# Masked attention in one kernel: scores kept in SBUF, row maxima spread by DMA, the mask as a bias

## The chip, the cores and the metric

The kernel runs on one core of a Trainium2 chip. The metric is the device time of one execution in microseconds. The core has five engines that run their own instruction streams and wait for each other by semaphores: TensorE (PE, with its weight loads PEld), VectorE (DVE), ScalarE (ACT), GpSimd (POOL) and SyncE (SP), which here only issues DMA transfers. Matrix products land in PSUM, which has eight banks of 128 partitions x 512 float32; everything else lives in SBUF. All data are float32.

## What is computed

Four layers follow each other, each added to its input x of shape 8 x 256 x 512: a masked attention (L0), a modulated attention (L1), an oscillator scan over 256 time steps (L2) and a GRU scan (L3). The change concerns the first, and where the result of the second is kept:

```python
def _L0_cond_ref(x, mask, Wq, Wo):          # x: B=8, D=256, T=512; mask: 8 x 512 of 0 and 1
    xt = jnp.transpose(x, (0, 2, 1))
    q = xt @ Wq.T
    qh = q.reshape(B, T, NH, dk).transpose(0, 2, 1, 3)           # 8 heads of 32
    scores = scale * jnp.einsum('bhqd,bhkd->bhqk', qh, qh)
    logits = (scores * cmask + (1.0 - cmask) * NEG) * rmask      # NEG = -1e30
    attn = jax.nn.softmax(logits, axis=-1)
    ctx = jnp.einsum('bhqk,bhkd->bhqd', attn, qh)
    out = ctx.transpose(0, 2, 1, 3).reshape(B, T, D) @ Wo.T
    return jnp.transpose(out, (0, 2, 1))
...
x = x + _L0_cond_ref(x, cond_2048, L0_cond_Wq, L0_cond_Wo)
x = x + _L1_cond_ref(x, cond_2048[:, None, :], ...)     # x after this line is called x2 below
x = x + _L2_cond_ref(cond_2048, cond_2048, x, ...)
x = x + _L3_cond_ref(cond_2048, x, ...)
```

Queries, keys and values are the same matrix, so the scores of a head are symmetric. A query row with mask 0 has logits that are all 0, and its result is the mean of all values.

## The kernel before

**Stages.** `tile_kernel` makes small constants, runs `attention` (L0 and L1 of all eight batch entries, interleaved), and then `scans` (L2 and L3). The scans need the weights `cT`, `wih`, `whh`, which `scan_weights` loads, and `x2T`, the result of L1 turned so that features lie on partitions. `x2T` is allocated at the top (L917), 32 KB of each partition, and lives through the whole kernel.

**Steps.** The attention is a software pipeline over steps g (L453 to L515), emitted in the order of the text; each engine runs its instructions in that order. A batch entry b takes U = 8 steps of masked work: two halves e of four heads each, and four steps per half. `at(g, rel, n)` says whether step g is the part number r of entry b at the offset rel; `heads(g, rel)` does so for the four head groups of the modulated attention. `norms`, `parts`, `HEADS` and `OUT` say at which steps an entry's normalization, qkv products, heads and output come.

**Masked attention of one half (b, e).** 
- `project` (steps -5 and -4): q for four heads into a bank; VectorE multiplies it by the mask row `mks` into `qm`, ScalarE copies it into `qt`, and `project_out` turns that on TensorE into `qtok`, the values. On GpSimd a line `neg` is made from the mask.
- `maxima0` (four steps from -4): for one block of 128 queries the scores of four heads over all 512 keys go into four banks (L204), and VectorE takes each row's maximum (L209) into `mxp0`. The condition is copied beside it by GpSimd (L195).
- `rows0`: TensorE turns `mxp0` into rows (L214), and ScalarE writes them, with signs, into `mrow` (L216).
- `weights0` (four steps from 0): the scores again, with keys on partitions, 256 queries at a time (L226), and a second product of depth 2, `neg` by `mrow`, that adds the mask term and subtracts the maximum in the bank (L231). ScalarE takes the exponential from PSUM into `ex` (L238).
- `values0`, in two parts, at steps 1 and 2: `ex` by the values, and `ex` by ones for the sums (both L153); `weigh0`: reciprocal (L163) and product (L164) into `ctxT`.
- `masked_out`: the output projection (L261), added to x on VectorE (L264).

**Modulated attention.** `normalize`, `modulate`, `qkv`, `qkv_norm`, `qkv_out`, `maxima1`, `rows1`, `weights1`, `values1`, `modulated_out`, and `modulated_turn`, which turns x2 on TensorE and copies it into `x2T` (L418). In `qkv_norm` VectorE sums squares (L322), GpSimd takes the power and multiplies (L324 to L326), and `qkv_out` of the next step turns the result. In `values1`, `weigh` follows at once.

**PSUM and queues.** `bank` hands out seven banks in rotation (`ps_s`), one more is for `values0` (`ps_c`). A product waits until the bank's last reader is done. Transfers are issued by SP in order: `load` brings x (four buffers) and the mask spread over 128 partitions, `mks` (one buffer). After step U*B+1 = 65 the pools of the masked attention are closed and `follow` issues the loads of the scan weights.

Of the kernel before, what the change touches and what calls it, by code (L numbers as in the profile page):

```python
# [24 lines left out]
def attention(ctx, tc, cst, x, cond, wqT, woT, w_emb, b_emb, g_norm, w_qkv, g_q, g_k, w_out, x2T, follow):  # L25
# [27 lines left out]
    ps_s = ctx.enter_context(tc.tile_pool(name="a_ps_s", bufs=7, space=PSUM))  # L53
# [7 lines left out]

    xs, mks = {}, {}

    def load(b):
        xs[b] = two.tile([P, 2, D], F32, tag="x", name=f"x_{b}", bufs=4)
        nc.sync.dma_start(xs[b], x[b].rearrange("(k p) t -> p k t", p=P))
        mks[b] = fone.tile([P, D], F32, tag="mk", name=f"mk_{b}")
        nc.sync.dma_start(mks[b], cond[b].partition_broadcast(P))
# [35 lines left out]

    rowm = wp.tile([P, 3], F32, name="rowm")
    nc.vector.memset(rowm, 0.0)
    nc.vector.memset(rowm[:, 1:2], 1.0)
    nc.vector.memset(rowm[:, 2:3], -1.0)
    for h in range(4):
        nc.vector.memset(rowm[32 * h : 32 * h + 1, 0:1], NEG)  # L110
        nc.vector.memset(rowm[32 * h : 32 * h + 1, 1:2], -NEG)
        nc.vector.memset(rowm[32 * h : 32 * h + 1, 2:3], 1.0)
# [54 lines left out]
    qms, qtoks, negs, mrows, exs0, ctxTs = {}, {}, {}, {}, {}, {}  # L167

    def project(b, e):
        if e == 0:  # L170
            qms[b] = ftwo.tile([P, 2, D], F32, tag="qm", name=f"qm_{b}")
            qtoks[b] = ftwo.tile([P, NJ, 256], F32, tag="qtok", name=f"qtok_{b}")
            negs[b] = ftwo.tile([P, D], F32, tag="neg", name=f"neg_{b}")
# [7 lines left out]
        nc.scalar.copy(qt, ps)  # L181
        if e == 0:
            nc.gpsimd.tensor_scalar(negs[b], mks[b], rowm[:, 0:1], rowm[:, 1:2], ALU.mult, ALU.add)
# [7 lines left out]

    def maxima0(b, e, qc):

        if qc == 0:
            nc.gpsimd.tensor_copy(  # L195
                mxp0[e].rearrange("p q (h i) -> p q h i", i=32)[:, :, :, 0],
                condT[:, :, b].unsqueeze(2).to_broadcast([P, NJ, 4]),
            )
        qm = qms[b]
        ss = []  # L200
        for h in range(4):
            r = 32 * h
            s = bank([P, D], f"n0_{b}_{e}_{qc}_{h}")
            nc.tensor.matmul(  # L204
                s, lhsT=qm[r : r + 32, e, qc * P : (qc + 1) * P], rhs=qm[r : r + 32, e, :], start=True, stop=True
            )
            ss.append(s)
        for h in range(4):
            nc.vector.tensor_reduce(mxp0[e][:, qc, 32 * h + 1 : 32 * h + 2], ss[h], AX.X, ALU.max)  # L209

    def rows0(b, e):
        pt = bank([P, NJ, P], f"pm0_{b}_{e}")
        for qc in range(NJ):
            nc.tensor.transpose(pt[:, qc, :], mxp0[e][:, qc, :], ident)  # L214
        mrows[b, e] = ftwo.tile([P, D], F32, tag="mrow", name=f"mrow0_{b}_{e}")
        nc.scalar.activation(mrows[b, e], pt.rearrange("p q n -> p (q n)"), AF.Copy, scale=rowm[:, 2:3])  # L216

    def weights0(b, e, qh, kp):
        qm, neg, mrow = qms[b], negs[b], mrows[b, e]
        qs = slice(256 * qh, 256 * qh + 256)  # L220
        ss = [bank([P, 2, 256], f"s0_{b}_{e}_{qh}_{kp}_{h}") for h in range(4)]
        for i in range(2):
            kc = slice((2 * kp + i) * P, (2 * kp + i + 1) * P)
            for h in range(4):
                r = 32 * h
                nc.tensor.matmul(  # L226
                    ss[h][:, i, :], lhsT=qm[r : r + 32, e, kc], rhs=qm[r : r + 32, e, qs], start=True, stop=False
                )
            for h in range(4):
                r = 32 * h  # L230
                nc.tensor.matmul(  # L231
                    ss[h][:, i, :], lhsT=neg[r : r + 2, kc], rhs=mrow[r : r + 2, qs], start=False, stop=True
                )
        exs = exs0.setdefault((b, e, qh), [])
        exs.append([])
        for h in range(4):
            ex = ftwo.tile([P, 2, 256], F32, tag="ex", name=f"ex0_{b}_{e}_{qh}_{kp}_{h}", bufs=12)
            nc.scalar.activation(ex, ss[h], AF.Exp, scale=SC)  # L238
            exs[-1].append(ex)

    pc0s = {}

    def values0(b, e, qh, half):
        if half == 0:
            if (e, qh) == (0, 0):
                ctxTs[b] = fone.tile([P, 2, D], F32, tag="ctxT", name=f"ctxT_{b}")
            pc0s[b, e, qh] = ps_c.tile([P, 2, 256], F32, tag="c", name=f"pc0_{b}_{e}_{qh}")
        pc = pc0s[b, e, qh]
        o = e * P
        values(pc, half, lambda k, h: qtoks[b][:, k, o + h * DH : o + (h + 1) * DH], exs0[b, e, qh])  # L250

    def weigh0(b, e, qh):
        pc = pc0s[b, e, qh]
        weigh(pc, ctxTs[b][:, e, qh * 256 : (qh + 1) * 256], f"0_{b}_{e}_{qh}")
# [159 lines left out]
    def modulated_turn(b, m, x2):  # L414
# [3 lines left out]
        nc.scalar.copy(x2T[:, :, b, m * P : (m + 1) * P], pt)  # L418
# [6 lines left out]
    for b in range(B):  # L425
        per = 2 if b >= B - 2 else 1
        norms.append(U * b + U + (1 if b == B - 1 else 2))
# [24 lines left out]
    with tc.manual_schedule():  # L452
        for g in range(-5, OUT[-1] + 3):  # L453
# [8 lines left out]
            if a := at(g, 0, U):  # L462
# [539 lines left out]
```

## Time and profile before

| | us |
|---|---|
| median of three runs | 3042.3 (3041.54 to 3044.32) |
| profiled execution | 3040.15 |
| its span, first to last instruction | 3038.4 |
| first product of the scans (L698) | 961.4 |
| first and last copy of masked rows (L216) | 24.5 and 783.4 |
| scan weights issued (L524) | 838.1 |

A row of the page's list of groups reads: line, engine, operation, result and operands by the names of the program, shapes and number; then busy time, the mean duration of one in ns; then the idle time of that engine before them and what ended it. A row of a timeline starts with its start and length in us. A row of a table of windows has the stretch and its length, then for PE, PEld, DVE, ACT and POOL the busy us and the number of instructions, then the granted TensorE clock (1.00 is full), the busy share of the 16 DMA engines and GB/s. "Entry" is a batch entry.

Some groups of the attention stage, by the same profile: L163 64 times 1750 ns, L164 64 times 424 ns, L238 256 times 603 ns, L209 256 times 683 ns, L325 32 times 2899 ns, L326 32 times 1047 ns, L363 32 times 399 ns.

### The profile page before, as it was taken

The page shows a single profiled execution, that of the slowest core. Times are in us where ns is not written, and L with a number is a line of the kernel's source. Part 1 is how long each engine was busy: PE and PEld are TensorE (multiplying, and loading weights), DVE is VectorE, ACT ScalarE, POOL GpSimd, SP SyncE. Part 2 cuts the span into 40 slices and gives each one's busy share as a digit, 9 for nine tenths or more (in the row PEclk, how much of TensorE's full clock was granted, in tenths as well). Part 3 has the DMA queues.
Part 4 walks back from the last instruction along what each step waited for, and adds up shares of the span by engine and source line. Part 5 has one row for each costly group of instructions (what it writes and reads, how often), then busy time and mean ns, then how long its engine had stood idle before and what let it go on. Part 6 is the DMA issues. An engine that isn't in the chain of part 4 may idle for free.

```text
span 3038.4 us, 165918 instructions
## 1 busy us (share of the span) xinstructions
PE 2847.2 (94%) x70330; PEld 2070.0 (68%) x70330; DVE 2002.5 (66%) x9090; ACT 1599.9 (53%) x8347; POOL 986.8 (32%) x2905
## 2 busy tenths in 40 slices
PE   8999999999988899999999999999999999999997
PEld 5455555555545677777777777777777777777775
DVE  4444444544434677777777777777777777777774
ACT  2333433433433566666666666666666666666652
POOL 0021111111221344444444444444444444444442
PEclk8999999999999999999999999999999999999999
DMA  3000000000040000000000000000000000000000
GB/s 129 5 1 1 12 11 1 12 11 1 2 98 2 4 7 6 7 6 6 7 6 7 6 6 7 6 7 6 6 7 6 7 6 6 7 6 7 6 6 7
DMA packets 17759, 35.31 MB, mean 12 GB/s; under 512 B 2144, under 2 KB 10860, under 8 KB 17012
## 3 DMA queue, kind: packets, MB, share of 16 engines
q1 hardware_dynamic: 17012, 24.69, 3.0%
q8 instruction: 550, 9.01, 1.2%
q14 instruction: 197, 1.61, 0.2%
HBM read 20.49 MB, written 4.19 MB: 8 GB/s over the span
## 4 chain that ended last, share of the span: by engine, by line
PE 62%; DVE 26%; ACT 6%; issue 4%; POOL 2%; ACTq 0%; DMA 0%; SPq 0%; POOLq 0%; DVEq 0%
PE pg L733 19%; PE ic L698 17%; PE psqkv L301 5%; DVE icT L890 5%; PE pc L153 5%; DVE qn L891 5%; ACT tT L598 4%; DVE hqs L851 3%; PE s L226 3%; DVE own L748 3%; DVE sqmm L847 2%; PE n L204 2%; DVE v L750 2%; PE psx L401 2%; DVE mxp L209 2%
## 5 line engine op out<-in xcount | busy, mean ns | idle before, releaser
L698 PE MATMUL ic<-cT_sb,tT 128*8 128x128 f32 x32736 | 1088.6, 273 | 82.2 <-ACT tT L598 44.6
L698 PEld LDWEIGHTS ic<-cT_sb,tT 128*8 128x8 f32 x32736 | 758.6, 89 | 344.0 <-ACT tT L598 272.0
L733 PE MATMUL pg<-whh_sb,hz 128*32 128x128 f32 x24576 | 818.5, 274 | 50.7 <-DVE hz L778 17.5
L598 ACT ACTIVATE tT<-qn 128x16 f32<-128x16 f32 x2046 | 440.2, 216 | 646.0 <-DVE qn L891 567.5
L733 PEld LDWEIGHTS pg<-whh_sb,hz 128*32 128x32 f32 x24576 | 667.4, 110 | 125.0 <-DVE hz L778 124.8
L890 DVE STREAM_TRANSPOSE icT<-ic 128x64 f32<-128x64 f32 x2048 | 503.7, 246 | 70.5 <-PE ic L698 64.9
L891 DVE SCALAR_TENSOR_TENSOR qn<-icT,hqs 128x16 f32<-128x16 f32 x2048 | 350.4, 171 | 70.1
L693 POOL TENSOR_TENSOR W<-W,cx 128x128 f32<-128x128 f32 x765 | 297.2, 389 | 256.7 <-ACT cx L679 256.7
L686 POOL TENSOR_TENSOR W<-cx,us 128x128 f32<-128x128 f32 x255 | 117.1, 459 | 446.1 <-ACT cx L679 446.1
L847 DVE SCALAR_TENSOR_TENSOR sqmm<-sqmm,qn 128x32 f32<-128x32 f32 x768 | 153.5, 200 | 152.2 <-ACT sqmm L836 123.1
L209 DVE TENSOR_REDUCE mxp<-n 128x1 f32<-128x512 f32 x256 | 158.7, 683 | 132.0 <-PE n L204 132.0
L851 DVE TENSOR_TENSOR hqs<-W,sqmm 128x32 f32<-128x32 f32 x1020 | 200.1, 196 | 46.1 <-DVE own L773 1.0
L238 ACT ACTIVATE ex<-s 128x512 f32<-128x512 f32 x256 | 132.1, 603 | 157.0 <-PE s L231 157.0
L712 PE MATMUL gi<-wih_sb,x3T 128*32 128x384 f32 (+2 forms) x3072 | 202.4, 379 | 0.5 <-POOL x3T L903 0.5
L324 POOL TENSOR_SCALAR r<-s 128x16 f32<-128x16 f32 x32 | 6.5, 204 | 604.0 <-DVE s L322 603.7
L679 ACT ACTIVATE cx<-qn 128x32 f32<-128x32 f32 x1280 | 200.9, 213 | 0.1
L301 PE MATMUL psqkv<-wqkv_sb,xnT 128*128 128x512 f32 x384 | 181.8, 620 | 0.0
L679 ACT ACTIVATE cx<-p 128x32 f32<-128x32 f32 x1020 | 149.8, 217 | 32.2 <-DVE p L846 1.4
L356 DVE TENSOR_REDUCE mxp<-n 128x2 f32<-128x512 f32 x128 | 79.6, 685 | 107.7 <-PE n L348 107.7
L226 PE MATMUL s<-qm 32*128 32x256 f32 x1024 | 139.4, 406 | 6.8 <-DVE mxp L209 6.8
L679 ACT ACTIVATE cx<-q 128x32 f32<-128x32 f32 x1020 | 145.5, 213 | 0.0
L748 DVE STREAM_TRANSPOSE own<-pg 128x128 f32<-128x128 f32 x256 | 84.9, 332 | 91.3 <-PE pg L733 91.3
(149 smaller groups left out, 3593.5 us busy)
## 6 DMA issues: line engine op xcount, KB each, us to landing
x<-in_x SPq DMA_DIRECT2D x8, 512.0 KB
out<-o SPq DMA_DIRECT2D x256, 16.0 KB
wqkv_sb<-in_L_cond_W_qkv SPq DMA_DIRECT2D x1, 3072.0 KB
wih_sb<-in_L_cond_W_ih SPq DMA_DIRECT2D x4, 768.0 KB
whh_sb<-in_L_cond_W_hh SPq DMA_DIRECT2D x4, 768.0 KB
mk<-in_cond SPq DMA_DIRECT2D x8, 256.0 KB
wemb<-in_L_cond_W_emb SPq DMA_DIRECT2D x4, 512.0 KB
wout_sb<-in_L_cond_W_out SPq DMA_DIRECT2D x1, 1024.0 KB
```

The source lines that it names most:

```text
L209: nc.vector.tensor_reduce(mxp0[e][:, qc, 32 * h + 1 : 32 * h + 2], ss[h], AX.X, ALU.max)
L226: nc.tensor.matmul(ss[h][:, i, :], lhsT=qm[r : r + 32, e, kc], rhs=qm[r : r + 32, e, qs], start=True, stop=False)
L301: nc.tensor.matmul(ps, lhsT=xnTs[b][:, c, m * P : (m + 1) * P], rhs=wqkv_sb[:, c, part * D : (part + 1) * D], start=(c == 0), stop=(c == N ...
L598: nc.scalar.activation(tT, src[:, half * HM : (half + 1) * HM, :], AF.Tanh)
L679: nc.scalar.activation(c[:, i], x, AF.Copy, scale=f)
L693: nc.gpsimd.tensor_tensor(W[:, i + 1 : 5], W[:, i + 1 : 5], c, ALU.add)
L698: nc.tensor.matmul(ps[32 * j : 32 * j + B, :], lhsT=tT[k // HM][:, k % HM, :], rhs=cT_sb[:, k, j * P : (j + 1) * P], start=(k == 0), stop= ...
L733: nc.tensor.matmul(pg_ps[rows(j), :], lhsT=hzs[tau % 3][:, k, 32 * g : 32 * g + 32], rhs=whh_sb[:, k, g, j * P : (j + 1) * P], start=((k, ...
L847: stt(mm, sq, LIN[s], qs, ALU.subtract, ALU.mult)
L851: nc.vector.tensor_sub(hq, W[:, s], mm)
L890: nc.vector.transpose(icT.rearrange("p m n -> p (m n)"), ic[:, half * 64 : half * 64 + 64])
L891: stt(qn[:, m2, :], icT[:, :, 0:B], IC[s], hq[:, m2, :], ALU.mult, ALU.add)
```

## The change

The masked attention makes its scores once. `scores0` computes them for 128 keys by 512 queries and four heads, and ScalarE copies them into an SBUF tile `sc` (six buffers of 8 KB per partition). Since they are symmetric, `maxima0` takes the row maxima from the same tile, in one instruction of 128 x 2048. `rows0` turns the maxima into rows as before, and then four transfers on SP each spread one row (from partition 0, 32, 64 or 96 of `mrow`) over 128 partitions, into `bc`. `weights0` subtracts `bc` from `sc` on VectorE, in place, and takes the exponential in SBUF, with the mask as a bias per key. `values0` runs one step later, per 128 keys, with 512 columns, into two banks of its own; six banks rotate in place of seven. `weigh0` guards the reciprocal, multiplies by the query mask and adds the mean of the values where the mask is 0, in two operations and a fill on GpSimd. The normalization of an entry comes one step later, and all that follows it.

`x2T` moves into the pool that is opened after the masked attention. Until it is there, `modulated_turn` writes x2 to DRAM, and after `follow` it is read back from there. `mk` gets two buffers. In the step, the maxima of both attentions stand in a new order.

```diff
+    negT = wp.tile([P, NJ, B], F32, name="negT")
+    nc.vector.tensor_scalar(negT, condT, NEG, -NEG, ALU.mult, ALU.add)
...
     def project(b, e):
...
         qt = line(f"qt_{b}_{e}")
-        nc.scalar.copy(qt, ps)
-        if e == 0:
-            nc.gpsimd.tensor_scalar(negs[b], mks[b], rowm[:, 0:1], rowm[:, 1:2], ALU.mult, ALU.add)
+        means[b, e] = sm.tile([P, 1], F32, tag="mean", name=f"mean_{b}_{e}")
+        nc.scalar.activation(qt, ps, AF.Identity, accum_out=means[b, e])
+        nc.gpsimd.tensor_scalar_mul(means[b, e], means[b, e], -1.0 / D)
...
+    def scores0(b, e, kc):
+        qm = qms[b]
+        ss = [bank([P, D], f"s0_{b}_{e}_{kc}_{h}") for h in range(4)]
+        for h in range(4):
+            r = 32 * h
+            nc.tensor.matmul(
+                ss[h], lhsT=qm[r : r + 32, e, kc * P : (kc + 1) * P], rhs=qm[r : r + 32, e, :], start=True, stop=True
+            )
+        sc = ftwo.tile([P, 4, D], F32, tag="sc", name=f"sc_{b}_{e}_{kc}", bufs=6)
+        for h in range(4):
+            nc.scalar.copy(sc[:, h, :], ss[h])
+        scs[b, e, kc] = sc
+
+    def maxima0(b, e, qc):
+        nc.vector.tensor_reduce(
+            mxp0[e].rearrange("p q (h i) -> p q h i", i=32)[:, qc, :, 0], scs[b, e, qc], AX.X, ALU.max
+        )
 
     def rows0(b, e):
         pt = bank([P, NJ, P], f"pm0_{b}_{e}")
         for qc in range(NJ):
             nc.tensor.transpose(pt[:, qc, :], mxp0[e][:, qc, :], ident)
-        mrows[b, e] = ftwo.tile([P, D], F32, tag="mrow", name=f"mrow0_{b}_{e}")
-        nc.scalar.activation(mrows[b, e], pt.rearrange("p q n -> p (q n)"), AF.Copy, scale=rowm[:, 2:3])
+        mrow = ftwo.tile([P, D], F32, tag="mrow", name=f"mrow0_{b}_{e}", bufs=1)
+        nc.scalar.copy(mrow, pt.rearrange("p q n -> p (q n)"))
+        bc = bcs[b, e] = ftwo.tile([P, 4, D], F32, tag="bc", name=f"bc_{b}_{e}")
+        for h in range(4):
+            nc.sync.dma_start(bc[:, h, :], mrow[32 * h : 32 * h + 1, :].unsqueeze(1).to_broadcast([1, P, D]))
+
+    def weights0(b, e, kc):
+        sc = scs[b, e, kc]
+        nc.vector.tensor_sub(sc, sc, bcs[b, e])
+        nc.scalar.activation(sc, sc, AF.Exp, bias=negT[:, kc, b : b + 1], scale=SC)
+
+    def values0(b, e, kc):
...
+        for half in range(2):
+            for h in range(4):
+                o = e * P + h * DH
+                nc.tensor.matmul(
+                    pc0s[b, e][half][32 * h : 32 * h + 32, :],
+                    lhsT=qtoks[b][:, kc, o : o + DH] if half == 0 else ones[:, 0:DH],
+                    rhs=sc[:, h, :], start=(kc == 0), stop=(kc == NJ - 1),
+                )
+
+    def weigh0(b, e):
+        fill = ftwo.tile([P, D], F32, tag="fill", name=f"fill_{b}_{e}", bufs=1)
+        nc.gpsimd.tensor_scalar(fill, mks[b], -1.0, means[b, e], ALU.add, ALU.mult)
+        cx = ctxTs[b][:, e, :]
+        pv, pn = pc0s[b, e]
         for i in range(2):
+            t = slice(256 * i, 256 * i + 256)
+            r = sm.tile([P, 256], F32, tag="r", name=f"r_0_{b}_{e}_{i}", bufs=2)
+            nc.vector.reciprocal(r, pn[:, t])
+            nc.vector.scalar_tensor_tensor(cx[:, t], r, 1e30, pv[:, t], ALU.min, ALU.mult)
+        nc.gpsimd.tensor_tensor(cx, cx, mks[b], ALU.mult)
+        nc.gpsimd.tensor_tensor(cx, cx, fill, ALU.add)
...
-        nc.scalar.copy(x2T[:, :, b, m * P : (m + 1) * P], pt)
+        if "x2T" in cst:
+            nc.scalar.copy(cst["x2T"][:, :, b, m * P : (m + 1) * P], pt)
+            return
+        o = line(f"x2o_{b}_{m}")
+        nc.scalar.copy(o, pt.rearrange("p j n -> p (j n)"))
+        x2d[b, m] = dram.tile([P, D], F32, name=f"x2d_{b}_{m}")
+        nc.sync.dma_start(x2d[b, m], o)
...
-        norms.append(U * b + U + (1 if b == B - 1 else 2))
+        norms.append(U * b + U + (2 if b == B - 1 else 3))
...
-            if a := at(g, 0, U):
-                weights0(a[0], a[1] // 4, a[1] // 2 % 2, a[1] % 2)
+            if a := at(g, 2, U):
+                values0(a[0], a[1] // 4, a[1] % 4)
+            if a := at(g, -4, U):
+                scores0(a[0], a[1] // 4, a[1] % 4)
+            if a := at(g, 1, U):
+                weights0(a[0], a[1] // 4, a[1] % 4)
...
-            if a := at(g, U + 1):
+            if a := at(g, U + 2):
                 masked_out(a[0])
...
-            a, a1 = at(g, -4, U), heads(g, 0)
-            soon = a and a[1] % 4 == 3
-            if a and soon:
+            if a := heads(g, 0):
+                maxima1(*a)
+            if a := at(g, -4, U):
                 maxima0(a[0], a[1] // 4, a[1] % 4)
-            if a1 and not soon:
-                maxima1(*a1)
...
+            if (a2 := at(g, 2, U)) and a2[1] % 4 == 3:
+                weigh0(a2[0], a2[1] // 4)
+            if a and a[1] % 4 == 3:
                 rows0(a[0], a[1] // 4)
...
-            if g == U * B + 1:
+            if g == U * B + 2:
                 first.close()
                 follow()
+                for (b, m), d in x2d.items():
+                    nc.sync.dma_start(
+                        cst["x2T"][:, :, b, m * P : (m + 1) * P], d.rearrange("p (j n) -> p j n", j=NJ)
+                    )
```

## The prediction

> **What bounds the kernel now.** I read the page's shares first, then the windows of 50 us, then the timelines of TensorE and of the transfer queue (SP) in one stretch of the attention, and last the windows of 2 and 3 us in which large loads run. The attention ends at 961 us (the first coupling product stands at 961.4 on TensorE); the scans after it are 2077 us long and keep their instructions.
>
> ```profile
> PE 2847.2 (94%) x70330; PEld 2070.0 (68%) x70330; DVE 2002.5 (66%) x9090; ACT 1599.9 (53%) x8347; POOL 986.8 (32%) x2905
> ...
> core 0: us, PE busy (x) PEld busy (x) DVE busy (x) ACT busy (x) POOL busy (x), PEclk, DMA share, GB/s
> 700.00:750.00 50.00, 48.18 (x469) 26.24 (x462) 23.10 (x31) 18.25 (x35) 12.61 (x10) 0.97 0.00 1
> ```
>
> In the attention TensorE is busy for 48 of 50 us, VectorE for 23, ScalarE for 18, GpSimd for 13. TensorE is the bound, and the DMA engines stand idle.
>
> ```profile
> 714.65 1.93 PE L153 MATMUL pc<-ex,ones 128*32 128x256 f32 x32
> 716.52 1.14 PE L204 MATMUL n<-qm 32*128 32x512 f32 x8
> ...
> 729.62 0.71 PE L226 MATMUL s<-qm 32*128 32x256 f32 x8
> 730.47 0.71 PE L231 MATMUL s<-mrow,neg 2*128 2x256 f32 x8
> 731.00 0.61 PE L226 MATMUL s<-qm 32*128 32x256 f32 x8
> 731.44 0.61 PE L231 MATMUL s<-mrow,neg 2*128 2x256 f32 x8
> ...
> 310.38 0.40 SPq L68 DMA_DIRECT2D mk<-in_cond  x1
> 422.81 0.37 SPq L66 DMA_DIRECT2D x<-in_x  x1
> ...
> 535.07 0.37 SPq L66 DMA_DIRECT2D x<-in_x  x1
> ...
> 647.70 0.37 SPq L66 DMA_DIRECT2D x<-in_x  x1
> ```
>
> The first lines are one step's masked attention: values (L153), scores for the maxima (L204), and the scores again with mask and maximum (L226, L231) from 729.62 to 732.05, 2.43 us; in steps with a short wait it is 2.9. The loads of x come once per batch entry, 422.81 to 535.07 to 647.70: 112.5 us for eight steps, 14.1 a step.
>
> **What the Trainium skill says.** "SBUF — State Buffer", section "Door 1: The DMA port swizzle", says that a transfer's rate depends on how many of 16 ports its partitions reach, some 27 GB/s each, and that partitions 0 and 32 lie on one port, 64 and 96 on another. The trace agrees for destinations. The scan weights (L524) go to 32 partitions at a time, 8 ports by that table; the weights before 34 us go to 128:
>
> ```profile
> 864.00:867.00 3.00, 3.00 (x35) 2.05 (x37) 0.95 (x2) 3.00 (x8) 0.00 (x0) 1.00 1.02 211
> 867.00:870.00 3.00, 3.00 (x56) 2.06 (x48) 3.00 (x4) 0.34 (x2) 0.00 (x0) 1.00 1.05 210
> ...
> 24.00:26.00 2.00, 2.00 (x17) 1.37 (x21) 0.00 (x0) 0.69 (x1) 0.21 (x1) 0.50 1.01 424
> 26.00:28.00 2.00, 2.00 (x27) 1.62 (x22) 0.00 (x0) 0.00 (x0) 0.00 (x0) 0.50 1.00 415
> ```
>
> In both all 16 engines are busy (share 1.0), but 32 partitions take 210 GB/s, 26 a port, and 128 take 420. So the port limits, not the engine. No transfer of this trace reads one SBUF partition. The same page, "Who interferes with whom", says that a VectorE instruction with two SBUF inputs and a GpSimd instruction that reads SBUF block each other; the trace has no long one of this kind.
>
> **The change, part by part.**
>
> Removed: L226 and L231, 64 calls at 2.4 to 2.9 us, about 21 us of TensorE per entry. The values product keeps its columns (512 instead of twice 256). TensorE's sum per entry falls from 112.5 to about 88 us, 11 a step.
>
> Added on VectorE: one subtraction of 128x2048 from two SBUF inputs per step. L164 gives 424 ns for 256 columns, the adds of 512 take 692, so 1.05 ns a column: 2.3 us ("VectorE: DVE Perf Modes", "The perf-mode tier table", has 2293 ns for it). The maximum of 2048 columns takes 2.3 us where four took 2.48. Per entry VectorE goes from some 53 to 70 us.
>
> Added on ScalarE: four copies out of PSUM, 2.1 us like the four exponentials of L238. The exponential becomes one of 2048 columns: 603 ns plus 1536 at 0.8 (L363 against L238), 1.9 us with its bias per partition. Some 15 us per entry.
>
> GpSimd: two means, a fill (0.8 us like L183) and two operations of 128x512 (1.05 each like L326) per half of an entry, less the mask line: +5 us per entry beside other work.
>
> SP: the x2 writes and reloads go beside other work. They stand behind the weight loads after step 66; weights 35 us at 208 GB/s and eleven reads of 256 KB some 10 more, in a tail that was 123 us from L524 to the scans: nothing, and 45 us if that cover were gone. The load of x now waits for an x2 add one step later, which is half a step ahead of its projection: 0 to 2 us four times, inside a step that waits for other work.
>
> PSUM: six rotating banks in place of seven, two for the values. It costs nothing while ScalarE empties banks in time; below, values1 waits once per entry for a bank whose copy stands behind the exponential, and the chain counts it.
>
> Added as a wait, and the one that decides: rows0 now ends in four transfers, each of which reads one 2 KB row of one partition 128 times, 256 KB. The first subtraction needs all four and is one step after: about 12 us. If a read is limited by its port as the writes above are, each takes 262 KB / 26 GB/s = 10.1 us. Two rows lie on one port and two on the other, but they are queued in this order on the same 16 engines, so I take them as serial: 40 us, 42 with issue and latency (the load of x at 310 shows about 1 us before bytes move). Bounds: 4.5 us if all 16 ports' rate were had (1 MB at 385 GB/s plus latency), 22 if the two ports overlapped, some 82 if one partition gave half a port. I take 42, as the only rate shown for a port is 26.
>
> Behind the waiting subtraction stand all VectorE work of that step (maxima, weighing, the x2 add), behind the exponential that waits for it ScalarE's copies, which free banks; TensorE stops within the step. The chain from landing to the next rows0, by steps modulo 8:
>
> First half of an entry (waits in step 1): subtraction 2.3; x2 add 0.7, maximum 2.3, sum of squares 0.7, weighing 4.4 (2 x 1.75 + 2 x 0.42): 10.4. GpSimd's fill and two products: 13. TensorE's output projection 3.6, qkv 3.6, W_out 3.6: 24. Then VectorE's x2 add, maximum and sum of squares 3.7, GpSimd 4.3 (0.2, 2.9, 1.05 and gaps): 32. Transposes, projection, modulated scores 3.8: 36. VectorE's maxima 2.5 and 2.3, rows and copy 1.4: 42. With the transfer, 84 us for four steps.
>
> Second half (waits in step 5): subtraction, exponential, v copy: 4.8; values1 at half clock (the trace grants 0.50 at 897 to 900 after an idle stretch) 3.4: 8.2; weighing of both kinds 6.6: 14.8; subtraction, exponential, copy 4.8: 19.6; values1 1.9, VectorE's maxima until 24, weighing 2.2: 26; subtraction 2.3, exponential behind the copies: 31; ScalarE's two copies and maxima row 1.6, scores 2.2, exponentials 2.1, row 0.6: 38. With the transfer, 80 us.
>
> So 164 us per entry instead of 112.5. From start: the first burst queues behind the weight loads, which end at 33 us; five short cycles while the pipeline fills, 57, 62, 67, 62 and 74 us (the same sums without the modulated work; the first is 42 and three steps of subtraction and maximum, 13.8, and the row); ten full ones, 820. The last rows0 comes at 1175, where it was at 783. The tail from there, 178 us, gets the last wait and loses some scores: +23. The scans start at 1376 instead of 961: +415. The profiled execution took 3040.15 us (span 3038.4 and 1.75 around it; the median shown is 3042.3). 3040 + 415 = **3455 us**. Ten us more or less in a cycle give 3340 to 3570.
>
> **Rivals.** (1) Faster: the transfers are hidden, because repeated reads of one row are not bound by a port. Then the same chains with 12 us in place of 42 give 104 us per entry, less cold clock perhaps 97; times 7.5 entries, 64 to 116 us saved: 2925 to 2975, about 2950. For it: the mask line mk, also one row read 128 times but from DRAM, lands fast (768 KB of x and mk in about 3 us at 311 to 314). Against it: that row isn't in SBUF. It decides below a burst of 16 us, where 164 - 2 x (42 - 16) reaches 112. (2) The two ports work at once: 22 us a burst, 16 x 20 us less than the forecast, 3135; against it the order of the queue. (3) One partition gives half a port: 82 us, 16 x 40 more, 4095; nothing in the trace speaks for it. (4) VectorE becomes the bound at 70 us per entry with blocking by GpSimd: below TensorE's 88, so only a part of rival 1's cost.
>
> **How the numbers follow.** Forecast 0.55; rival 1 0.25; rival 2 0.12; rival 3 0.04; other 0.04. The likeliest case's own range is 3340 to 3570. Leaving out rivals 1 and 3 would leave out more than two in ten, so the range goes down to rival 1's faster end: 2930 to 3570, which leaves out some 0.15. About 0.2% is what a measurement can tell from no change. Faster 0.25, same 0.01, slower 0.74.
>
> **What would show it.** Right: windows of some 40 us per burst in which the DMA share is 1 and the rate 26 GB/s; VectorE's longest wait is the subtraction's, on the transfer, 16 times about 30 us; TensorE idle in each; L226 and L231 gone. Wrong: the subtraction waits for ScalarE or for nothing, the rate in the burst is over 75 GB/s, or the period per entry is below 112 us. If the wait is 10 us long, rival 2 holds; if TensorE waits for GpSimd's normalization instead, my chains matter and not the transfers.

## The result and the profile after

| | before | after |
|---|---|---|
| median of four runs, us | 3042.16 (3041.54 to 3044.32) | 3518.76 (3518.33 to 3519.49) |
| ratio | 1 | 1.1565, 95% interval 1.1545 to 1.1585 |
| span of the profiled execution, us | 3038.4 | 3517.6 |
| mean granted TensorE clock | 0.986 | 0.906 |
| first product of the scans, us | 961.4 | 1441.9 |

The changed kernel is 476 us slower. The scans are as long as they were (3517.6 - 1441.9 = 2076 us, before 2077), so all of the loss lies in the attention. On the page, the shares of the engines, the first part of the chain that ended last, and the group of the subtraction (line, operation, shapes and number, then busy us and mean ns, then idle time before it and who ended it):

```profile
PE 2758.9 (78%) x67258; PEld 1939.2 (55%) x67258; DVE 2127.4 (60%) x8948; ACT 1720.3 (49%) x8427; POOL 1089.4 (31%) x2945
...
PE 44%; DVE 26%; DMA 13%; ACT 7%; issue 4%; SPq 3%; POOL 2%; ACTq 0%; DVEq 0%; POOLq 0%
...
L225 DVE TENSOR_TENSOR sc<-sc,bc 128x2048 f32<-128x2048 f32 x64 | 146.8, 2294 | 441.6 <-DMA bc<-mrow 441.6
```

TensorE works 88 us less than before and still falls from 94% to 78% of the span. A transfer, the spread row, now holds 13% of the chain. VectorE stood idle for 441.6 us ahead of the subtraction. The waits up to 1440 us name the rest (engine, instruction, what it waited for; total us, times, longest):

```profile
POOL r L327 <- DVE s L325: 481.1, 28, 33.9
DVE sc L225 <- DMA bc<-mrow: 441.6, 16, 32.0
POOL ctxT L256 <- DVE ctxT L255: 419.7, 10, 63.0
ACT sc L226 <- DVE sc L225: 387.1, 18, 30.4
...
PE pc L237 <- DVE ctxT L255: 172.8, 15, 33.3
PE ptx L420 <- DVE x L409: 121.1, 11, 23.2
PE pc L154 <- ACT vt L314: 114.1, 5, 23.2
```

The largest sums, GpSimd's, belong to an engine that is 31% busy and cost nothing by themselves. The line that counts is the second: sixteen waits, one per half of an entry, all for the spread row, 27.6 us on average. ScalarE's exponential passes the wait on, and TensorE meets it as waits for VectorE and ScalarE. The same burst in windows of 4 us (columns as in the tables of windows before):

```profile
802.00:806.00 4.00, 3.43 (x36) 0.96 (x28) 2.69 (x3) 0.76 (x3) 3.24 (x3) 1.00 0.86 26
810.00:814.00 4.00, 4.00 (x11) 1.71 (x9) 0.00 (x0) 0.00 (x0) 0.00 (x0) 1.00 0.88 26
814.00:818.00 4.00, 0.49 (x2) 0.00 (x0) 0.00 (x0) 0.00 (x0) 0.00 (x0) 1.00 0.89 43
818.00:822.00 4.00, 0.00 (x0) 0.00 (x0) 0.00 (x0) 0.00 (x0) 0.00 (x0) 0.62 0.90 27
826.00:830.00 4.00, 0.00 (x0) 0.00 (x0) 0.00 (x0) 0.00 (x0) 0.00 (x0) 0.50 0.91 27
838.00:842.00 4.00, 0.78 (x4) 0.38 (x2) 3.66 (x3) 3.01 (x5) 1.07 (x2) 0.50 0.00 0
```

Through most of the burst all 16 DMA engines are some nine tenths busy and move 26 to 28 GB/s, but for one window with 43 in the middle. By the order of the queue, that is where the row of partition 64 follows that of partition 32. From about 815 to 834 us no compute engine does anything, and TensorE's clock falls to one half. Last, the transfer queue (start, length, operation, number; the length of the row transfers is the time in which SP issues the four, not the time in which they land):

```profile
694.30 0.39 SPq L74 DMA_DIRECT2D x<-in_x  x1
...
795.83 17.77 SPq L221 DMA_DIRECT2D bc<-mrow  x4
861.97 0.39 SPq L74 DMA_DIRECT2D x<-in_x  x1
...
965.79 17.77 SPq L221 DMA_DIRECT2D bc<-mrow  x4
...
1032.26 0.39 SPq L74 DMA_DIRECT2D x<-in_x  x1
```

From one load of x to the next it is 167.7 and 170.3 us per entry, where it was 112.5. The last burst is issued at 1218.1.

### The profile page after: what moved, and what is told of

Read it like the earlier page. It is cut to its first block, busy times and chain, and to the rows that moved or that the text cites. A ratio compares the mean times of both kernels' runs of the same rounds, so it can differ in the third digit from the quotient of the medians.

```text
span 3517.6 us, 159950 instructions
## 1 busy us (share of the span) xinstructions
PE 2758.9 (78%) x67258; PEld 1939.2 (55%) x67258; DVE 2127.4 (60%) x8948; ACT 1720.3 (49%) x8427; POOL 1089.4 (31%) x2945
## 4 chain that ended last, share of the span: by engine, by line
PE 44%; DVE 26%; DMA 13%; ACT 7%; issue 4%; SPq 3%; POOL 2%; ACTq 0%; DVEq 0%; POOLq 0%
PE pg L737 16%; PE ic L702 15%; DMA bc<-mrow 13%; DVE icT L894 4%; DVE qn L895 4%; SPq L221 3%; ACT tT L602 3%; DVE hqs L855 3%; PE psqkv L304 3%; DVE own L752 2%; PE pc L237 2%; DVE sqmm L851 2%; DVE v L754 2%; DVE r L254 2%; PE pc L154 1%
## 5 line engine op out<-in xcount | busy, mean ns | idle before, releaser
L225 DVE TENSOR_TENSOR sc<-sc,bc 128x2048 f32<-128x2048 f32 x64 | 146.8, 2294 | 441.6 <-DMA bc<-mrow 441.6
L226 ACT ACTIVATE sc<-sc,negT 128x2048 f32<-128x2048 f32 x64 | 129.5, 2024 | 421.9 <-DVE sc L225 387.1
L237 PE MATMUL pc<-sc,qtok 128*32 128x512 f32 x512 | 91.8, 798 | 224.4 <-DVE ctxT L255 172.8
L203 ACT COPY sc<-s 128x512 f32<-128x512 f32 x256 | 131.7, 602 | 237.0 <-PE s L198 237.0
L208 DVE TENSOR_REDUCE mxp<-sc 128x4 f32<-128x2048 f32 x64 | 145.8, 2281 | 57.4 <-ACT sc L203 57.4
L327 POOL TENSOR_SCALAR r<-s 128x16 f32<-128x16 f32 x32 | 20.3, 635 | 481.4 <-DVE s L325 481.1
L256 POOL TENSOR_TENSOR ctxT<-ctxT,mk 128x512 f32<-128x512 f32 x16 | 37.6, 2351 | 419.7 <-DVE ctxT L255 419.7
```

Source lines behind the costliest of these rows:

```text
L237: nc.tensor.matmul(pc0s[b, e][half][32 * h : 32 * h + 32, :], lhsT=qtoks[b][:, kc, o : o + DH] if half == 0 else ones[:, 0:DH], rhs=sc[:, ...
```

## Experiments

Two questions were open. Is it the transfer that costs the time? And if it is taken away, is the rest faster than the kernel before, as the first rival had it? All times are medians, and a ratio is the time of the run by that of the kernel before, with its 95% interval; the kernel before took 3041.7 to 3044.7 us beside them.

### The transfer taken away in three ways, and halved

**e1_dram**: the row goes to DRAM first and is spread from there.

```diff
+        row = dram.tile([4, D], F32, name=f"row_{b}_{e}")
         for h in range(4):
-            nc.sync.dma_start(bc[:, h, :], mrow[32 * h : 32 * h + 1, :].unsqueeze(1).to_broadcast([1, P, D]))
+            nc.sync.dma_start(row[h : h + 1, :], mrow[32 * h : 32 * h + 1, :])
+        for h in range(4):
+            nc.sync.dma_start(bc[:, h, :], row[h].partition_broadcast(P))
```

> The four maxima rows are written to DRAM (2 KB each) and spread from there, as mk is. Theory P (a read of one SBUF partition gets one port's 26 GB/s, so a burst of four takes 40 us): a burst from DRAM takes about 3 us of data and two latencies, some 7 us in all, inside the 12 us before the first subtraction, so the subtraction waits for almost nothing: 2950 us (2900 to 3010). Rival N (it is the count of transfers or descriptors, 512 per burst, not where they read): the same burst, 3500. Rival V (the subtraction, its conflicts with GpSimd and the new order of the step cost the time, the transfers only look late): 3450 to 3520.

Measured: 3168.96 us, ratio 1.0414 (1.0396 to 1.0431). The windows of one burst, whose issue begins at 644.64 us:

```profile
644.00:648.00 4.00, 4.00 (x20) 2.55 (x23) 1.66 (x1) 3.10 (x6) 0.00 (x0) 0.50 0.25 48
648.00:652.00 4.00, 4.00 (x24) 1.30 (x17) 0.00 (x0) 1.63 (x4) 0.00 (x0) 0.96 0.62 216
652.00:656.00 4.00, 2.66 (x36) 1.98 (x38) 3.11 (x6) 3.17 (x5) 0.90 (x2) 1.00 0.00 0
```

The same megabyte lands within 8 us of its issue, at up to 216 GB/s, and all 64 subtractions together wait 4.2 us for it. Removing the slow read takes 350 us off. So the transfer was the cause of most of the loss, and it was reading one partition of SBUF that made it slow, not writing 128. But the kernel is still some 127 us slower than the kernel before: the 2950 of the first rival does not come with a fast transfer alone.

**e2_two**: only the rows of heads 0 and 1 are spread, and heads 2 and 3 are given the same two rows; so half of the maxima stay unused.

```diff
-        for h in range(4):
+        for h in range(2):
...
-        nc.vector.tensor_sub(sc, sc, bcs[b, e])
+        two = bcs[b, e][:, 0:2, :].unsqueeze(1).to_broadcast([P, 2, 2, D])
+        nc.vector.tensor_sub(
+            sc.rearrange("p (i h) t -> p i h t", i=2), sc.rearrange("p (i h) t -> p i h t", i=2), two
+        )
```

> Only the rows of heads 0 and 1 are spread; heads 2 and 3 subtract those, so the maxima of half the heads are left out. Theory P: a burst is 20 us instead of 40, the wait before each of the 16 first subtractions falls from some 28 to 8 us, 3518 - 16 x 20 = 3200 us. Rival V: 3518. If the time is fixed per burst and not per row: 3518.

Measured: 3245.68 us, ratio 1.0668 (1.0646 to 1.0689). The subtraction waits 16 times, 164.5 us in all, 10.3 on average instead of 27.6. Half of the bytes of a burst, 17 us less of wait: the time follows the bytes, and is not fixed per burst. (Half as many are read and half as many written here; which of the two counts is what e1_dram shows.)

**e3_rep**: GpSimd repeats each maximum in 32 columns ahead of the transposes, so that a row stands in 32 partitions, and sixteen transfers go from 32 partitions to 32.

```diff
+        m4 = mxp0[e].rearrange("p q (h i) -> p (q h) i", i=32)
+        nc.gpsimd.tensor_copy(m4[:, :, 1:32], m4[:, :, 0].unsqueeze(2).to_broadcast([P, 16, 31]))
...
+        for c in range(4):
+            for h in range(4):
+                nc.sync.dma_start(bc[32 * c : 32 * c + 32, h, :], mrow[32 * h : 32 * h + 32, :])
```

> GpSimd repeats each maximum over 32 columns, so that after the turn 32 partitions hold a head's row; sixteen transfers of 64 KB per burst then go from 32 partitions to 32. Still SBUF to SBUF, the same bytes. Theory P: 8 ports are read, 210 GB/s, 5 us of data, bound by 16 issues of 0.45 us on SP, about 9 us in all: hidden, 2970 us (2910 to 3040). Rival S (any transfer that reads SBUF is slow, one port or many): 3500. Rival N: no better than 3500.

Measured: 3238.63 us, ratio 1.0644 (1.0623 to 1.0666). With 32 source partitions the burst runs at 99 to 108 GB/s and is over within 12 us of its issue. The 70 us above e1_dram have a place of their own, the added copy. TensorE waits for it at the turn of the maxima:

```profile
PE pm L218 <- POOL mxp L215: 98.0, 16, 8.6
```

In e1_dram the wait at the same place, for VectorE's last maximum, is 38.8 us. The 59 us more, and 18.4 us of wait for the rows instead of 4.2, come to about the difference.

**e4_pe**: no transfer at all; TensorE multiplies each row by ones at the start of the next step, and ScalarE copies the four banks into `bc`.

```diff
+            nc.tensor.matmul(ss[h], lhsT=ones[r : r + 1, :], rhs=mrow[r : r + 1, :], start=True, stop=True)
...
-            nc.sync.dma_start(bc[:, h, :], mrow[32 * h : 32 * h + 1, :].unsqueeze(1).to_broadcast([1, P, D]))
+            nc.scalar.copy(bc[:, h, :], ss[h])
```

> No transfers for the maxima: one step later TensorE multiplies a column of ones by each row (four products of 128x512, packed by rows, 1.2 us a burst) and ScalarE copies them into bc (2.1 us). Theory P: 16 x 1.2 us of TensorE, no wait: 2950 us (2900 to 3010), with TensorE waiting for GpSimd's normalization in some steps. Rival V: 3450 to 3520.

Measured: 3225.76 us, ratio 1.0599 (1.0583 to 1.0615), 136.5 us per entry where e1_dram has 126.3. The products keep TensorE busy for some 2.5 us per half of an entry, twice what was expected and 39 us in all; the rest of the 57 us above e1_dram was not followed. Three different ways without the slow read end between 3169 and 3239, and in all three TensorE still waits about 100 us for the weighing of the half before (101.9, 99.6 and 101.9 us): something else holds the kernel above 3042.

### What holds e1_dram above the kernel before

TensorE's timeline in e1_dram, its longest waits of one entry (in brackets: idle us, and what ended it):

```profile
607.23 1.93 PE L240 MATMUL pc<-sc,qtok 128*32 128x512 f32 x8 [6.40 <-DVE ctxT L258]
...
632.77 1.11 PE L342 MATMUL ptqk<-ident,qr 128*128 128x128 f32 x4 [5.52 <-POOL qr L332]
643.52 0.48 PE L216 MATMUL pm<-ident,mxp 128*128 128x128 f32 x1 [4.28 <-DVE mxp L208]
...
676.85 1.94 PE L240 MATMUL pc<-sc,qtok 128*32 128x512 f32 x8 [7.23 <-DVE ctxT L258]
```

L240 is `values0` of a new half. Its two banks still hold the sums of the half before, until `weigh0` (L258) has read them, and `weigh0` is the last of VectorE's work in its step, behind the x2 add, the maxima and the norm's sum of squares. After each wait the first products take 1.94 us instead of 1.06 (624.26, without a wait): twice the time, as at half clock. L342 waits for GpSimd's normalization, whose sum of squares now stands behind the 2.3 us maximum; L216 waits for the last maximum before the rows, which stands behind that of the modulated attention.

**e5_weigh**: `weigh0` is emitted right behind `weights0`.

```diff
                 weights0(a[0], a[1] // 4, a[1] % 4)
+            if (a2 := at(g, 2, U)) and a2[1] % 4 == 3:
+                weigh0(a2[0], a2[1] // 4)
...
-            if (a2 := at(g, 2, U)) and a2[1] % 4 == 3:
-                weigh0(a2[0], a2[1] // 4)
```

> As e1_dram (rows spread from DRAM, 3169 us), but weigh0 is emitted right behind weights0 instead of last among the step's VectorE work. Bank theory: what is left over in e1_dram is mainly the wait of each half's first values product for weigh0 of the half before (6.4 and 7.2 us per entry), and the half clock that follows it; with weigh0 ahead of the x2 add, maxima and norm sums these two waits shrink to about 1 us: 16 x (6 + 2) = 130 less, 3020 to 3060. Rival, VectorE-bound: the work is only reordered on an engine that is the limit, and another wait on VectorE takes the place; 3150 to 3190.

Measured: 3108.9 us, ratio 1.0215 (1.0198 to 1.0232): 60 us less than e1_dram, where 110 to 150 were expected. **e6_order** puts the maxima back into the order of the kernel before as well:

```diff
-            if a := heads(g, 0):
-                maxima1(*a)
-            if a := at(g, -4, U):
-                maxima0(a[0], a[1] // 4, a[1] % 4)
+            a, a1 = at(g, -4, U), heads(g, 0)
+            soon = a and a[1] % 4 == 3
+            if soon:
+                maxima0(a[0], a[1] // 4, a[1] % 4)
+            elif a1:
+                maxima1(*a1)
             for part, lines in made:
...
+            if a and not soon:
+                maxima0(a[0], a[1] // 4, a[1] % 4)
+            if a1 and soon:
+                maxima1(*a1)
```

> As e5_weigh, and the maxima of masked attention stand behind the norm's sum of squares (in the step of rows0 ahead of everything), as in the kernel before. Bank theory: the waits for GpSimd's normalization (5.5 and 2.7 us) and for the last maxima before rows0 (4.3 us) shrink as well, some 8 us per entry: 60 to 100 less than e5_weigh, 2930 to 2990, faster than the kernel before. Rival: same as e5_weigh within 20 us, because VectorE and GpSimd together are full.

Measured: 3013.15 us, ratio 0.9895 (0.9878 to 0.9912), 1% faster than the kernel before. The step from e5_weigh, 96 us, is what was expected; the time is above the 2930 to 2990 put down for it, because e5_weigh had gained less. TensorE's waits of the whole attention, in e1_dram:

```profile
PE pc L240 <- DVE ctxT L258: 101.9, 15, 8.8
PE ptqk L342 <- POOL qr L332: 64.6, 18, 5.5
PE pm L216 <- DVE mxp L208: 38.8, 12, 4.3
```

in e5_weigh:

```profile
PE ptqk L342 <- POOL qr L332: 96.9, 24, 5.5
PE pm L216 <- DVE mxp L208: 38.8, 12, 4.3
...
PE pc L240 <- DVE ctxT L258: 4.3, 1, 4.3
```

and in e6_order:

```profile
PE ptqk L342 <- POOL qr L332: 55.4, 24, 3.9
...
PE pm L216 <- DVE mxp L208: 19.6, 11, 4.0
```

e5_weigh removes 98 us of the first wait and hands 32 back to the second: the sum of squares now waits behind `weigh0`, and GpSimd's small step after it comes to lie beside a subtraction more often (L330 takes 1064 ns on average instead of 695). That leaves 66, which is about the 60 that came; the half clock behind each wait, for which another 2 us had been put down, did not bring its share. e6_order shortens both that are left. The rival, that VectorE is the limit and only changes places, does not hold. In 500 to 800 us of e6_order VectorE is busy for 197.8 us and TensorE for 264.5, and the time fell.

**e11_out** takes up the wait that is left, for GpSimd's normalization: the transposes of a normalized part move behind the qkv product of their step. **e12_head** does the same except in the step in which the heads start.

```diff
+            if heads(g, 0) and heads(g, 0)[1] == 0:
+                for a in leave("qkv"):
+                    qkv_out(*a)
             if a := at(g, -5, 2):
...
             made = [(part, qkv(*part)) for part in parts.get(g, ())]
+            for a in leave("qkv"):
+                qkv_out(*a)
```

(the old place, ahead of the projections, goes; the first three lines are e12_head's alone)

> As e6_order (3013 us), with the transposes and copies of a normalized part emitted behind the qkv product of their step instead of ahead of the projections. If the wait for GpSimd's normalization (2.2 us in most steps) is what is left on TensorE: 3013 - 60 x 1.5 = 2910 to 2970. Rival, that wait is covered by nothing else and something of VectorE or ScalarE takes its place: 2995 to 3030.

> As e11_out (2986 us), but in the one step of an entry in which the modulated heads start, the transposes of the last normalized part stay ahead of the projections, since the scores of that step need their copies at once (TensorE waits there 5.3 us in e11_out, once an entry). If that wait only changes place: 2980 to 2990. If the early place covers it: 8 x 3 to 8 x 5 less, 2945 to 2965.

Measured: e11_out 2986.09 us, ratio 0.9811 (0.9796 to 0.9826), less gained than expected: from 300 us on TensorE waits five times for ScalarE's copy of those transposes, 24.0 us in all. e12_head 2962.87 us, ratio 0.9747 (0.9730 to 0.9763), as expected where the early place covers that wait, and the fastest of all. Its loads of x are 95.4 us apart:

```profile
310.49 0.38 SPq L74 DMA_DIRECT2D x<-in_x  x1
405.93 0.38 SPq L74 DMA_DIRECT2D x<-in_x  x1
501.47 0.38 SPq L74 DMA_DIRECT2D x<-in_x  x1
```

### The same order with the slow transfers kept

**e8_weigh_after** makes e5_weigh's move in the changed kernel, **e10_order_after** both moves of e6_order (the diffs are the same two).

> The changed kernel, its SBUF transfers kept, with weigh0 emitted right behind weights0. Transfer theory: the 42 us burst sets the chain, and weigh0 is one link of the 42 us that follow it; taking 3.7 us of other VectorE work ahead of it out twice an entry gives at most 16 x 4 to 16 x 6 less: 3420 to 3460. If the value banks were a cost of their own size and added to the transfers in full: 3519 - 130 = 3390. If weigh0 is off the chain while transfers set it: 3519.

> The changed kernel, its SBUF transfers kept, with both new orders of e6_order. Transfer theory: the order now takes out only what lies in the two chains of 42 us behind a burst (the maxima of the modulated attention ahead of the last masked ones, 2.5 us, twice an entry, and the waits for GpSimd's normalization, some 5 us an entry): 3420 to 3470. If order and transfers add in full: 3519 - 156 = 3363. If the order is worth nothing beside the transfers: 3500.

Measured: e8_weigh_after 3503.55 us (ratio 1.1508, 1.1491 to 1.1526), e10_order_after 3428.96 us (1.1269, 1.1252 to 1.1286). The first takes off 15 us, where the transfer theory had 64 to 96, and comes out nearest to the case in which `weigh0` is off the chain; the second lies where the transfer theory put it. Two lines of the first one's table of waits, TensorE's:

```profile
PE ptx L420 <- DVE x L409: 143.1, 12, 27.5
...
PE pc L237 <- DVE ctxT L255: 103.1, 4, 31.3
```

The wait for `weigh0` falls from 172.8 to 103.1 us and that for the x2 add rises from 121.1 to 143.1; normalization rises from 57.1 to 79.0. Everything on VectorE stands behind the same stalled subtraction, and putting one piece ahead of another there moves the wait. Both moves together take off 90 us beside the slow transfers and 156 without them: the two costs overlap and are not a sum.

### Two queues, and one part alone

**e9_queues**: the rows of partitions 64 and 96 go by ScalarE's queue.

```diff
         for h in range(4):
-            nc.sync.dma_start(bc[:, h, :], mrow[32 * h : 32 * h + 1, :].unsqueeze(1).to_broadcast([1, P, D]))
+            (nc.sync if h < 2 else nc.scalar).dma_start(bc[:, h, :], mrow[32 * h : 32 * h + 1, :].unsqueeze(1).to_broadcast([1, P, D]))
```

> The changed kernel, with the rows of heads 2 and 3 (partitions 64 and 96) issued on ScalarE's queue and those of heads 0 and 1 (partitions 0 and 32) on SP's. Port theory: the two pairs lie on two ports, and two queues let both work at once: the burst runs at some 52 GB/s for 20 to 24 us instead of 26 GB/s for 40, the wait of the first subtraction falls to about 13 us, and the time to that of e2_two, 3245, plus up to 50 for ScalarE held while it issues: 3200 to 3320. Rival, one limit for all reads of single partitions, or for the engines: the rate stays at 26 to 28 GB/s and the time at 3500 to 3560.

Measured: 3372.59 us, ratio 1.1084 (1.1065 to 1.1102). The wait of the subtraction, and two windows of a burst that is issued at 627.3:

```profile
DVE sc L225 <- DMA bc<-mrow: 211.8, 16, 23.1
...
630.00:634.00 4.00, 3.17 (x22) 0.70 (x14) 0.00 (x0) 0.00 (x0) 0.00 (x0) 0.84 0.91 27
...
646.00:650.00 4.00, 4.00 (x22) 1.56 (x15) 0.00 (x0) 2.46 (x5) 0.00 (x0) 1.00 0.81 60
```

Neither theory has all of it. The wait is what the port theory put, 13.2 us on average, and the rate reaches 60 GB/s, so there is no single limit of 27 for all such reads. But it does so only towards the end of the burst, which takes 28.9 us from issue to subtraction (627.30 to 656.22) instead of 38.8 or the 20 to 24 expected, and the time is above the 3200 to 3320 of that theory. ScalarE is held for 7.6 us by each pair of issues but the first; how much of the time this accounts for was not separated. Nor does this run tell whether the port or the queue matters: each queue had its own port. Two rows of one port on two queues were not tried, and neither was one queue with the partitions in the order 0, 64, 32, 96.

**e7_x2only**: the kernel before, with x2 by way of DRAM and `x2T` in the later pool.

```diff
-    x2T = cp.tile([P, NJ, B, T], F32, name="x2T")
...
+            cst["x2T"] = pool.tile([P, NJ, B, T], F32, name="x2T")
...
-        nc.scalar.copy(x2T[:, :, b, m * P : (m + 1) * P], pt)
+        if "x2T" in cst:
+            nc.scalar.copy(cst["x2T"][:, :, b, m * P : (m + 1) * P], pt)
+            return
+        o = line(f"x2o_{b}_{m}")
+        nc.scalar.copy(o, pt.rearrange("p j n -> p (j n)"))
+        x2d[b, m] = dram.tile([P, D], F32, name=f"x2d_{b}_{m}")
+        nc.sync.dma_start(x2d[b, m], o)
```

(and the reads behind `follow`, as in the change)

> The kernel before with one part of the change alone: x2 goes by way of DRAM and x2T moves into the later pool. My forecast's step says it costs nothing: 3042, within 6 us either way. Rival: the reads stand late behind the weight loads and hold up the scans: up to 45 us more, 3087.

Measured: 3045.46 us beside 3044.72, ratio 1.0002 (0.9993 to 1.0010): nothing, as the forecast's step had it.

## Why the prediction was right, and where it was not

**The deciding step held.** The forecast named the four reads of one partition, their rate, and the wait they would end in. It put 26 GB/s, 42 us from issue to landing and about 30 us of wait sixteen times. The trace has 26 to 28 GB/s, 38.8 us (795.83 to the subtraction at 834.65) and 27.6. e1_dram, which changes only where the row is read from, takes 350 us off. The rate of a port, from writes to many partitions, was the right price for reads of one; there was some luck in this, as no transfer of the trace before read a single partition, and the forecast took the only rate that it had. That it is a port and not the partition that limits is supported, and not proved. In windows of 1 us, the first one of data left out, the rate goes above 31 GB/s only at 815 to 817 (47 and 72) and, in the same half of the next entry, at 985 to 987 (53 and 68): half-way, where partition 64 takes over from 32, which the forecast had on another port. Where 32 takes over from 0, on the same port, no rise is seen.

**The sum was 64 us short** (3455 for 3518.8), and the terms that were mis-sized are the chains between landing and the next rows. The forecast had 42 and 38 us; in the entry shown they are 48.7 (834.65 to 883.32) and 43.7 (922.13 to 965.79). The two transfers, each 3 us shorter than forecast, hid half of that, so that an entry takes 170 us and not 164. The first chain, from the timeline:

```profile
834.65 2.29 DVE L225 TENSOR_TENSOR sc<-sc,bc 128x2048 f32<-128x2048 f32 x1 [29.72 <-DMA bc<-mrow]
...
844.58 0.42 DVE L255 SCALAR_TENSOR_TENSOR ctxT<-r,pc 128x256 f32<-128x256 f32 x1
844.92 2.39 DVE L225 TENSOR_TENSOR sc<-sc,bc 128x2048 f32<-128x2048 f32 x1
845.15 2.72 POOL L248 TENSOR_SCALAR fill<-mk,mean 128x512 f32<-128x512 f32 x1
...
849.18 1.27 POOL L257 TENSOR_TENSOR ctxT<-ctxT,fill 128x512 f32<-128x512 f32 x1
850.75 3.60 PE L264 MATMUL pso<-ctxT,wo_sb 128*128 128x512 f32 x8
...
861.25 0.69 DVE L409 TENSOR_TENSOR x<-psx,x 128x512 f32<-128x512 f32 x1 [6.17 <-PE psx L404]
...
864.65 2.29 DVE L225 TENSOR_TENSOR sc<-sc,bc 128x2048 f32<-128x2048 f32 x1
864.82 2.17 POOL L327 TENSOR_SCALAR r<-s 128x16 f32<-128x16 f32 x1 [14.38 <-DVE s L325]
...
871.17 1.12 PE L339 MATMUL ptqk<-ident,qr 128*128 128x128 f32 x4 [5.53 <-POOL qr L329]
...
877.46 2.49 DVE L359 TENSOR_REDUCE mxp<-n 128x2 f32<-128x512 f32 x4 [1.03 <-PE n L351]
```

Link by link: weighing ends at 845.0, 10.4 us after landing, exactly as forecast. GpSimd's fill and products end at 850.45, 15.8 instead of 13: the fill, 0.8 us in the forecast, starts a quarter of a microsecond after a subtraction and takes 2.72. The three products on TensorE and VectorE's part then take the forecast's time, but GpSimd's first small step takes 2.17 us instead of 0.2, again beside a subtraction. From the transposes at 871.17 to the modulated maxima at 877.46 it is 6.3 us where 3.8 were put down. These three, 2.8, 2.0 and 2.5, make up the 6.7, the other links being half a microsecond shorter. The forecast named the blocking of GpSimd by an instruction with two SBUF inputs, from the Trainium skill's "SBUF — State Buffer", section "Who interferes with whom", and set it at a part of rival 4, not in its own chain. The page says that the later of the two waits for the whole instruction; the trace agrees, with 2.17 us for one of 0.20.

In the second chain, weighing ends 15.1 us after landing (forecast 14.8). Then the exponential and the v copy behind it should end at 19.6 and end at 24.9 (946.98), since ScalarE's copies stand ahead of them and the scores for these behind a `values0` that waited 4.2 us for its two banks:

```profile
937.27 1.93 PE L237 MATMUL pc<-sc,qtok 128*32 128x512 f32 x8 [4.20 <-DVE ctxT L255]
...
946.37 0.61 ACT L314 COPY vt<-psqkv 128x512 f32<-128x512 f32 x1
```

That wait was nowhere in the forecast.

Over the kernel, the last rows come at 1218.1 instead of 1175. Of these 43 us the ten full cycles account for 22.8 (375.30 to 1218.10 is 842.8 us, forecast 820) and the five short ones for 25.6 (347.6 instead of 322), less 5.3 because the first burst is issued at 27.7 and not at 33. The tail to the scans is 223 us where 178 + 23 = 201 were forecast; it has one wait of 29.3 us for the modulated row behind the exponential (L374 for L366) and one of 8.0 for GpSimd, and the kernel before has neither. The range of the forecast, 115 us to either side, held the result; but ten us in each of its fifteen cycles would be 150, so it was narrower than the reason given for it.

**The first rival did not come.** The transfers were not hidden. Nor would hiding them have been enough: its period of 97 to 104 us per entry, and its time of 2950, assumed that nothing but the transfer was in the way, and that a change with a burst below 16 us pays. With a burst of 8 us the period was 126.3 (e1_dram) and the kernel slower than before. What the step missed: two value banks without a second pair, released by the last work of VectorE's queue; and two maxima that had been put ahead of what the next step waits for. With both moved, the period is 99 to 102 (e6_order), with the normalized transposes moved 95.4, and the time 2963. That this lies in the rival's range is no merit of the rival, which had none of these moves.

**The small steps.** L226 and L231 are gone; TensorE's busy time fell by 88 us in all, and not by 21 an entry, which would be 168; in e12_head, with the clock back at 0.980, it fell by 148, so that much of the gap seems to go with the clock. The subtraction takes 2294 ns (2.3 forecast), the maximum 2281 (2.3), the exponential 2024 (1.9). The way over DRAM costs nothing, with the reads at 1335 us well ahead of the scans at 1442; e7_x2only measures it alone. VectorE (rival 4) was not the bound. Two ports at once (rival 2) is what e9_queues comes nearer to with two queues; from one queue they hardly overlapped, as the forecast took it. Half a port for one partition (rival 3) is ruled out by the 26 to 28 GB/s.

## What to carry to other kernels

Price a broadcast in a transfer by what it reads, too: four rows, each of one SBUF partition and read 128 times, gave 27 GB/s here, the same rows from DRAM up to 216. So look for the smallest number of partitions on either side before the bytes. When a wait is removed on paper, walk the step once more and ask of each buffer without a second copy which instruction releases it, and how far back in its engine's queue that stands; here that was worth 60 us and the order of the maxima 96 more, together the difference between slower and faster. Reordering work that stands behind one stalled instruction moved the waits and gained 15 us; the same move gained 60 once the stall was gone.

## What was not expected of the hardware

- SP does not only queue transfers: four that each read one partition hold it for 17.8 us (795.83), while two are issued in 1.1 us in e2_two (558.30) and eight to and from DRAM within 3 us in e1_dram (644.64). In e9_queues ScalarE was held for 7.6 us by its pair of such transfers, while SP's pair of the same burst was issued in 1.1 us (777.52). Work behind such an issue waits too: ScalarE's next copy stood idle for 7.66 us at 634.94.
- GpSimd's small operations can grow by most of the length of a subtraction beside them: L327 took 635 ns on average where the same operation took 204 before, L256 2351 where it takes 1268 in e6_order. e5_weigh and e6_order also changed which of GpSimd's steps lie beside a subtraction: the first step of the normalization took 695 ns on average in e1_dram, 1064 in e5_weigh and 264 in e6_order. This may be part of what they gained or lost; it was not separated.
- The clock is part of the price of a wait. The Trainium skill's "TensorE: Matmul & The Clock Gate", section "What's actually happening", says that the array falls to half clock after an idle window of about 3.4 us and needs as long a busy one to come back. The trace agrees: with TensorE idle from about 815 us the clock fell between 818 and 822, stood at 0.50 from 822 to 846, and was full again from about 850, some 5 us after TensorE's work began at 845.15. The first `values0` took 1.94 us at that clock instead of 1.06; the mean clock fell from 0.986 to 0.906 and came back to 0.980 in e12_head.
- Two queues were not equal to one here. The Trainium skill's "DMA: Bandwidth & Descriptors", section "Issuing engines are not separate DMA queues", says that a second issuing engine only saves issue time, as all run on the same 16 engines. In e9_queues the same four reads, split over two queues, went from 27 to as much as 60 GB/s and took 146 us off the kernel; the measurement decides for this kind of read. Whether it is the second queue or only the order of the ports that did it stays open, as said above.
